# A mixer's second gate product moved to the third block of tokens, and its norm behind the fourth block's gates

## The chip, the cores and the metric

The kernel runs on one core of a Trainium2 chip. The metric is the device time of one execution in microseconds, as a median of several runs; a profile is taken of one further execution. Engines are named as in the profile: PE (TensorE, with PEld for its weight loads), DVE (VectorE), ACT (ScalarE), POOL (GpSimd), SP (SyncE, which only issues DMAs here).

## The reference: what is computed

The kernel is a decoder of six blocks in a row, each followed by a residual sum and a layer norm: a mixer with a state space, a cross attention, a quantized feed-forward part, a causal attention, a recurrent decoder with 128 steps, and a feed-forward part with binary weights. The change touches the first block alone. There the input (16 x 128 tokens of 1024) is projected down to 128, and the same mixer is applied twice in a row, blended with its input, and projected up again. The mixer, cut to what matters:

```
zxbcdt = u @ in_w.T
z, xBC, dt2 = split(zxbcdt)                 # 256, 288, 2 x 4
dt_fw, dt_bw = softplus(dt2 + dt_bias)      # forward and backward in time
xBC = silu(causal_conv(xBC, conv_w, conv_b))            # 7 taps
xs, Bm, Cm = split(xBC)                     # 256, 16, 16
y = shifted scan forward + shifted scan backward        # 16 steps of time
y = y + xs * repeat(xs @ fcD_w.T + D, 64)               # the gate's first product
yz = y * silu(z)                                        # the gate's second product
y = yz * rsqrt(mean(yz ** 2) + 1e-5) * norm_w           # the norm
return y @ out_w.T
```

The scan is over 16 steps, so it is computed as a masked product: for each block of 128 tokens (8 sequences of 16 steps) a 128 x 128 matrix of weights is made for each of 4 heads and multiplied with xs.

## The kernel before, in words

`stage_hydra` cuts the 2048 tokens into 4 quarters of 512 and applies the mixer twice to each: 8 items. They run in 10 rounds of a software pipeline, `for n in range(10)` (line 437). In round n three items are in work: item n is entered (its projections, convolutions and gates: the functions in `first`), item n-1, `inner`, has its four blocks of 128 tokens weighed and summed (`mx.weights(inner, j)`, `mx.summed(inner, j)`), and item n-2, `outer`, is ended (the functions in `last`). The softplus of item n+1 is made by `coming[1]()`. Rounds 2 to 7 hold all three kinds, round 7 without a softplus, round 8 has no item to enter, round 9 only an ending.

The names that matter, with lines of the kernel before:

- `first[0]`, `first[1]`, `first[2]` (`convolved`, lines 249 to 263): a projection by PE (L254), a copy and a scaled copy by ACT (L256, L258), and six steps of the convolution by DVE (L263). They make bc, the first half of xs and the second half of xs.
- `first[3]` (`gates`): the decays by PE (L242), exp by ACT (L244), a sum and a product by POOL (L246, L247), three silus by ACT (L283), two projections by PE with silu by ACT (L287, L288), and the padded copy cpad by POOL (two settings to zero, L291 and L292, and a copy, L293).
- `steps` (`coming[1]`): four small matmuls (L220), the softplus on DVE (L222, L167 to L186, one exp on ACT, L169), and two products by POOL, rf (L234).
- `weights(j)`: two matmuls (L306), masks and their sum by DVE (L308, L310), the weights wt by DVE (L312), two transposes by PE (L316) and a copy xtok by ACT (L318).
- `summed(j)`: four matmuls with wt and xtok (L327) and a copy into y by ACT (L328).
- `last[0]` and `last[1]` are `gated(0)` and `gated(1)`, for the two halves of the 256 channels. `last[2]` is `norm`, `last[3]` projects (L369) and spreads the root over 128 columns (L362, copied by ACT, L364), `last[4]` multiplies the two by DVE (L418, which makes h, the input of the second pass; in the last four endings L426 and a sum by POOL, L427).

```
def gated(c):
    ...
    pf = self.acc()
    for kc in range(2):
        nc.tensor.matmul(pf, w["fc"][...], xs[:, kc, :], start=(kc == 0), stop=(kc == 1))   # L340
    tt = self.t([P, 512], "tt")
    nc.vector.scalar_tensor_tensor(tt, pf, w["D"][:, c:c + 1], xs[:, c, :], ALU.add, ALU.mult)  # L343
    nc.gpsimd.tensor_tensor(tt, tt, y[:, c, :], ALU.add)                                      # L344
    nc.vector.tensor_tensor(y[:, c, :], tt, s["zs"][:, c, :], ALU.mult)                       # L345
    nc.scalar.activation(s["sq"][:, c, :], y[:, c, :], AF.Square)                             # L346
```

`norm` is eight matmuls of a 128 x 128 block of sq with one column of ones (L353; the profile counts 16, as it counts float32 matmuls by passes), one activation by ACT (L355) and one power by POOL (L356). All matmuls here are float32.

What sets the order of the work: `K.ordered` (closed by `order()` at the end of the stage) binds PE and ACT to the order in which the code issues their instructions. DVE and POOL are not bound in this stage; the build orders each of their queues by itself, as it finds operands ready, and that order is then fixed in the program. Each engine runs its queue strictly in order. PSUM has three buffers of 128 x 512 (`acc`) and four of 128 x 256 (`small`), which go round in the order of the code; cpad has two buffers.

Of the kernel before, what the change touches and what calls it, by code (L numbers as in the profile page):

```python
# [69 lines left out]
def column(v):  # L70

    return v.rearrange("(p o) -> p o", o=1)


def spread(v, parts=P):

    return v.rearrange("(o n) -> o n", o=1).to_broadcast([parts, v.shape[0]])
# [301 lines left out]
def stage_hydra(K, xmid, ahead):  # L379

    nc, a = K.nc, K.a
    with ExitStack() as st:
        keep = K.pool(st, "h_keep")
        work = K.pool(st, "h_work")
        ps = K.pool(st, "h_ps", 1, PSUM)
        wdn = K.t(keep, [P, 8, P], "wdn")
        nc.scalar.dma_start(wdn, a["w_downT"].rearrange("(k p) d -> p k d", p=P))
        bdn = K.t(keep, [P, 1], "bdn")
        nc.scalar.dma_start(bdn, column(a["b_down"]))
        xt = []  # L390
        for q in range(4):
            xt.append(K.t(work, [P, 8, 512], "xt", bufs=2))
            for h in range(2):
                nc.sync.dma_start(xt[q][:, 4 * h:4 * h + 4, :],
                                  a["xT"][512 * h:512 * h + 512, q * 512:(q + 1) * 512].rearrange("(k p) n -> p k n", p=P))
            if q == 0:
                w = hydra_weights(K, keep)
        al = K.t(keep, [P, 3], "al")
        nc.scalar.dma_start(al[:, 2:3], spread(a["gate1"]))
        nc.scalar.activation(al[:, 2:3], al[:, 2:3], AF.Sigmoid)  # L400
        nc.vector.tensor_scalar(al[:, 0:1], al[:, 2:3], -1.0, 1.0, ALU.mult, ALU.add)
        nc.vector.tensor_scalar(al[:, 1:2], al[:, 2:3], 1.0, None, ALU.add)
        w["eps"] = K.t(keep, [P, 1], "eps")
        nc.vector.memset(w["eps"], 1e-5)
        mx = Mixer(K, w, work, ps)

        def down(q):
            ph = mx.acc()
            for k in range(8):
                nc.tensor.matmul(ph, wdn[:, k, :], xt[q][:, k, :], start=(k == 0), stop=(k == 7))  # L410
            u = K.t(keep, [P, 512], f"u{q}")
            nc.scalar.activation(u, ph, AF.Gelu, bias=bdn)
            return u

        def between(q):
            def put(po, rr):
                h = h1[q] = K.t(keep, [P, 512], f"h{q}")
                nc.vector.tensor_tensor(h, po, rr, ALU.mult)  # L418
            return put

        def blended(q):
            def put(po, rr):

                t = mx.t([P, 512], "tt")
                nc.scalar.activation(t, u[q], AF.Copy, scale=al[:, 1:2])
                nc.vector.scalar_tensor_tensor(rr, po, al[:, 0:1], rr, ALU.mult, ALU.mult)  # L426
                nc.gpsimd.tensor_tensor(xmid.rearrange("p (l j s) -> p j l s", l=HY_L, s=8)[:, 4 * q:4 * q + 4],  # L427
                                        rr.rearrange("p (j l s) -> p j l s", l=HY_L, s=8),
                                        t.rearrange("p (j l s) -> p j l s", l=HY_L, s=8), ALU.add)
            return put  # L430

        u, h1 = [None] * 4, [None] * 4
        order = K.ordered((mybir.EngineType.Activation, mybir.EngineType.PE))
        inner = outer = None
        for n in range(10):
            s, first = None, []
            ahead(n, mx.acc)
            if n == 0:  # L440
                u[0] = down(0)
                coming = mx.entry(u[0])
                coming[1]()
            if n < 8:
                s, _, first = coming
            if n < 7:
                if n < 3:
                    u[n + 1] = down(n + 1)
                coming = mx.entry(u[n + 1] if n < 3 else h1[n - 3])
            last = []  # L450
            if outer is not None:
                m = n - 2
                last = mx.ending(outer, between(m) if m < 4 else blended(m - 4))
            for j in range(4):
                if last and j < 2:
                    last[j]()
                if inner is not None:
                    mx.weights(inner, j)
                    if j:
                        mx.summed(inner, j - 1)  # L460
                if last and j == 2:
                    last[2]()
                if first:
                    first[j]()
                if n < 7 and j == 1:
                    coming[1]()
                if last and j == 3:
                    last[3]()
            if inner is not None:
                mx.summed(inner, 3)  # L470
            if last:
                last[4]()
            inner, outer = s, inner
        order()
# [1315 lines left out]
def decoder_kernel(tc, a, out):  # L1790
    nc = tc.nc
    K = Ctx(tc, a)
    with ExitStack() as st:
# [11 lines left out]
        with ExitStack() as s1:  # L1805
            xmid = K.t(K.pool(s1, "xmid", side="right"), [P, NT], "xmid")
            rise = Rise(K, K.pool(s1, "c_ahead", side="right"))
            got = []
            steps = {4: lambda bank: rise.load(), 5: lambda bank: got.append(quant_vectors(K, fkeep)), 6: lambda bank: rise.fetch(0),
                     7: lambda bank: rise.fetch(1), 8: rise.fold}  # L1810
            stage_hydra(K, xmid, lambda n, bank: steps[n](bank) if n in steps else None)
            slab = K.pool(st2 := st.enter_context(ExitStack()), "f_w")
            with ExitStack() as s2:
                wf, piece = quant_weights(K, slab, K.pool(s2, "f_raw", 2))
                stage_cross(K, rise, xmid, x1, piece)
# [154 lines left out]
```

## Time and profile before

| what | value |
|---|---|
| median of 3 runs | 3191.89 us (3186.04 to 3192.75) |
| profiled execution, its own time | 3192.77 us |
| its span | 3191.0 us, 70103 instructions, mean clock of TensorE 0.968 |
| round 2 of the mixer stage | 92.47 to 120.40 us of the span |
| round 3 | 120.40 to 149.53 us |
| round 4 | 149.53 to 177.25 us |
| round 5 | 177.25 to 204.96 us |
| round 6 | 204.96 to 232.94 us |
| round 7 | 232.94 to 261.39 us |
| round 8 | 261.39 to 283.63 us |
| first matmul of the next stage | 303.12 us |

A round is counted here from the first matmul of `gated(0)` (L340) to that of the next round. The mixer stage is the first 303 us of the span, a tenth of it; the rest is the five other blocks of the decoder.

How to read it: lines of the profile give the kernel's line number, the engine, the operation, the tiles (output <- inputs), shapes and, in a timeline, the start in microseconds of the span, the duration, and in square brackets how long the engine had been idle before and what released it. "Granted clock" is the share of full speed at which TensorE was clocked. A timeline merges equal instructions that follow each other (x16 is sixteen of them).

### The profile page before, as it was taken

What the parts mean: (1) busy time and instruction counts of PE and PEld (TensorE: products, weight loads), DVE (VectorE), ACT (ScalarE), POOL (GpSimd) and SP (SyncE); (2) the same over time, 40 slices, a digit from 0 to 9 for tenths busy, and PEclk for the clock granted to TensorE, in tenths of its full rate; (3) what the DMA queues carried; (4) which work ended last, traced back from release to release, by engine and by line L of the source; (5) the groups of instructions that cost most, each with busy time, mean ns of one, the idle gap of its engine ahead of it and who ended that gap; (6) DMA issues with size and microseconds to landing.
All of it is one profiled execution on the core that took longest, in us unless ns stands there. A gap on an engine that the chain in (4) does not pass through costs nothing. (4 is left out here: it accounts for less than half of the span.)

```text
span 3191.0 us, 70103 instructions
## 1 busy us (share of the span) xinstructions
PE 2875.3 (90%) x28549; PEld 1615.9 (51%) x28549; DVE 1782.1 (56%) x5099; ACT 1499.6 (47%) x3606; POOL 878.0 (28%) x1096
## 2 busy tenths in 40 slices
PE   6998788799899999999998888888888888888898
PEld 2555455588555555555544444444444444444465
DVE  5785777577244554554434555555555555555555
ACT  3453433455133434442425555555555555565533
POOL 3223755477343333331110111110111111110222
PEclk8887999899999999999999999999999999999999
DMA  5000321221400101024212000101010000000244
GB/s 208 1 1 22 117 71 64 82 70 67 180 27 27 53 26 42 27 66 126 90 38 70 12 22 25 32 25 32 25 32 25 25 19 25 19 19 16 69 112 99
DMA packets 96525, 168.08 MB, mean 53 GB/s; under 512 B 14282, under 2 KB 55115, under 8 KB 96203
## 3 DMA queue, kind: packets, MB, share of 16 engines
q1 hardware_dynamic: 92138, 154.47, 15.2%
q10 hardware_dynamic: 4064, 9.11, 0.7%
q8 instruction: 226, 3.70, 0.5%
q14 instruction: 97, 0.79, 0.1%
HBM read 113.21 MB, written 51.64 MB: 52 GB/s over the span
## 5 line engine op out<-in xcount | busy, mean ns | idle before, releaser
L1177 ACT ACTIVATE th<-pf 128x1024 f32<-128x1024 f32 x381 | 254.2, 740 | 277.2 <-PE pf L1162 277.1
L1305 POOL COPY hist<-gT 128x16 f32<-128x16 f32 x256 | 42.4, 197 | 895.2 <-DVE gT L1304 895.2
L1277 PE MATMUL s<-hb,aD 128*32 128x256 f32 x4096 | 266.9, 387 | 7.9 <-DVE aD L1265 1.0
L854 PE MATMUL p<-xT,ga_Wq 128*128 128x512 f32 x512 | 226.4, 599 | 3.5 <-DMA ga_Wq<-ga_Wq 3.5
L1259 ACT COPY pf<-enc 128x512 f32<-128x512 f32 x381 | 225.5, 592 | 8.0
L928 PE MATMUL p<-ga_Wo,cT 128*128 128x512 f32 x512 | 222.5, 593 | 0.0
L1162 PE MATMUL pf<-R,waf 32*128 32x160 f32 x2032 | 181.4, 426 | 33.7 <-DVE R L1328 33.7
L894 ACT ACTIVATE s<-s,nm 128x128 f32<-128x128 f32 x512 | 197.5, 387 | 27.0 <-DVE nm L891 27.0
L897 POOL TENSOR_TENSOR s<-s,rs 128x512 f32<-128x512 f32 x128 | 133.0, 1039 | 251.7 <-DVE rs L896 246.7
L909 ACT COPY pT<-p 128x512 f32<-128x512 f32 x64 | 37.5, 586 | 269.9 <-PE p L906 269.9
L854 PEld LDWEIGHTS p<-xT,ga_Wq 128*128 128x128 f32 x512 | 96.4, 191 | 132.7 <-issue 119.3
L1195 DVE TENSOR_REDUCE nm<-s 128x1 f32<-128x128 f32 x128 | 37.3, 292 | 219.5 <-PE s L1181 219.5
L928 PEld LDWEIGHTS p<-ga_Wo,cT 128*128 128x128 f32 x512 | 97.1, 190 | 122.3 <-issue 120.5
L1181 PE MATMUL s<-th,vaE 128*32 128x128 f32 x2048 | 82.4, 279 | 78.8 <-ACT th L1177 78.7
L1277 PEld LDWEIGHTS s<-hb,aD 128*32 128x32 f32 x4096 | 95.1, 110 | 109.2 <-DVE aD L1265 86.7
L1297 ACT ACTIVATE fs<-ff,rx 128x384 f32<-128x384 f32 x127 | 73.7, 580 | 147.4 <-DVE rx L1295 147.4
L1162 PEld LDWEIGHTS pf<-R,waf 32*128 32x128 f32 x2032 | 79.3, 182 | 99.3 <-DVE R L1328 74.1
L1181 PE MATMUL ff<-th,vaE 128*32 128x128 f32 x2048 | 108.8, 285 | 8.0
L1109 PE MATMUL p<-ys,qT 128*128 128x512 f32 x256 | 112.3, 595 | 0.1
L1312 PE MATMUL gq<-gs,gT 128*32 128x128 f32 x2032 | 81.8, 279 | 31.8 <-DVE gT L1304 31.8
L95 POOL TENSOR_TENSOR ln_rs<-ln_ve,neghalf 128x1 f32<-128x1 f32 x64 | 37.9, 595 | 261.4 <-DVE ln_ve L89 251.0
L929 DVE TENSOR_TENSOR x<-p,x 128x512 f32<-128x512 f32 x32 | 22.1, 692 | 156.1 <-PE p L928 156.1
(396 smaller groups left out, 6631.3 us busy)
## 6 DMA issues: line engine op xcount, KB each, us to landing
x<-x SPq DMA_DIRECT2D x106, 512.0 KB, 3.6
xt<-xT SPq DMA_DIRECT2D x8, 1024.0 KB, 8.1
x<-x ACTq DMA_DIRECT2D x16, 512.0 KB, 2.6
x<-x SPq DMA_DIRECT2D x128, 64.0 KB, 2.3
xb<-r SPq DMA_DIRECT2D x16, 512.0 KB, 3.0
xb<-xb SPq DMA_DIRECT2D x16, 512.0 KB, 3.9
out<-xb SPq DMA_DIRECT2D x128, 64.0 KB, 2.7
ga_Wo<-ga_Wo SPq DMA_DIRECT2D x2, 2048.0 KB, 12.8
```

Source lines behind the costliest of these rows:

```text
L854: nc.tensor.matmul(pq, lhsT, xT[:, k].rearrange("p i t -> p (i t)"), start=(k == 0), stop=(k == 7))
L894: nc.scalar.activation(s[:, r, :], s[:, r, :], AF.Exp, bias=nm[:, r:r + 1], accum_out=sm[:, r:r + 1])
L897: nc.gpsimd.tensor_tensor(s, s, rs.unsqueeze(2).to_broadcast([P, 4, P]), ALU.mult)
L928: nc.tensor.matmul(po, cT[:, k, :], w["o"][h][:, k, :], start=(k == 0), stop=(k == 7))
L1109: nc.tensor.matmul(py, xT[:, k, b % 4, :], ys[:, k, :], start=(k == 0), stop=(k == 7))
L1162: nc.tensor.matmul(pf[:, k, first:first + n].rearrange("p b t -> p (b t)"), lhs[32 * k:32 * k + 32, :], rhs[32 * k:32 * k + 32, 32 * first ...
L1177: nc.scalar.activation(th.rearrange("p i (k t) -> p i k t", t=32), terms[:, :, first:first + n, :].rearrange("p k i t -> p i k t"), AF.Tanh)
L1181: nc.tensor.matmul(pe[32 * i:32 * i + 32, :], D["va"][:, 31 - b:63 - b], th[:, j, :], start=False, stop=(b % 8 > 3), skip_group_check=True)
L1259: nc.scalar.copy(pf[:, k], D["enc"][:, k])
L1277: nc.tensor.matmul(pg[32 * i:32 * i + 32, :], aD[:, 4 * g + i, :], D["hb"][:, 4 * g + i, :], start=(g == 0), stop=(g == 3), skip_group_che ...
L1297: nc.scalar.activation(fs.rearrange("p c t -> p (c t)"), ff[:, 0:3 * P], AF.Copy, scale=rx)
L1312: nc.tensor.matmul(gq[32 * q:32 * q + 32, :], gT[:, c].rearrange("p e b -> p (e b)"), D["gs"][:, c, q * P:(q + 1) * P], start=False, stop= ...
```

## The change

The diff moves calls in the loop over the four blocks of a round; no instruction is added or taken away.

```
             for j in range(4):
-                if last and j < 2:
-                    last[j]()
+                if last and j in (0, 2):
+                    last[j // 2]()
                 if inner is not None:
                     mx.weights(inner, j)
                     if j:
                         mx.summed(inner, j - 1)
-                if last and j == 2:
-                    last[2]()
                 if first:
                     first[j]()
                 if n < 7 and j == 1:
                     coming[1]()
-                if last and j == 3:
-                    last[3]()
+            if last:
+                last[2]()
             if inner is not None:
                 mx.summed(inner, 3)
             if last:
+                last[3]()
                 last[4]()
```

- The second gate product, `gated(1)`, is issued at the head of block j = 2 and no longer at the head of block j = 1.
- The norm is issued behind the fourth block's `gates`, and no longer between the third block's sum and the third convolution.
- The projection and the spreading of the root come behind the fourth block's sum, and no longer ahead of it.

On PE a round thus runs, before: gate 0, block 0, bc projection, gate 1, block 1, sum 0, xs projection, softplus input, block 2, sum 1, norm, xs projection, block 3, sum 2, decays, two z projections, output projection, root spread, sum 3. And after: gate 0, block 0, bc projection, block 1, sum 0, xs projection, softplus input, gate 1, block 2, sum 1, xs projection, block 3, sum 2, decays, two z projections, norm, sum 3, output projection, root spread. In rounds 8 and 9 the same holds for the parts that they have.

In the built programs DVE and POOL take other orders too. On DVE the steps of the softplus move up among the convolution's steps, L343 and L345 of the second gate stand behind most of the convolutions of bc and of the first half of xs, and L308 of the third and fourth block follow that L345. On POOL the zeroing of the next cpad (L291, L292), which stood behind both gates' L344 and ahead of the power, now stands between the two L344; the products rf (L234) come ahead of the copy into cpad (L293); and the power (L356) is the last of a round. SP's queue keeps its order.

More of the change, by code (lines that the diff above doesn't have):

```diff
@@ L454, in stage_hydra @@
             for j in range(4):
-                if last and j < 2:
-                    last[j]()
+                if last and j in (0, 2):
+                    last[j // 2]()
                 if inner is not None:
@@ L460, in stage_hydra @@
                         mx.summed(inner, j - 1)
-                if last and j == 2:
-                    last[2]()
                 if first:
@@ L466, in stage_hydra @@
                     coming[1]()
-                if last and j == 3:
-                    last[3]()
+            if last:
+                last[2]()
             if inner is not None:
@@ L471, in stage_hydra @@
             if last:
+                last[3]()
                 last[4]()
```

## The prediction

> **What bounds the kernel now.** I read the page's first part, then the mixer stage cut into rounds, then one round as a timeline, then the clock in short windows. The page says that TensorE is the busy engine of the whole kernel:
>
> ```profile
> PE 2875.3 (90%) x28549; PEld 1615.9 (51%) x28549; DVE 1782.1 (56%) x5099; ACT 1499.6 (47%) x3606; POOL 878.0 (28%) x1096
> ```
>
> The change lies in the mixer stage alone, so I cut that into its rounds (a round starts with the first matmul of L340). Columns: time and instructions of PE, PEld, DVE, ACT, POOL, then the granted clock.
>
> ```profile
> 149.53:177.25 27.72, 25.73 (x116) 14.81 (x114) 23.16 (x54) 13.73 (x28) 7.49 (x10) 0.82 0.00 1
> 177.25:204.96 27.71, 26.12 (x116) 15.19 (x115) 23.15 (x54) 13.85 (x28) 7.84 (x11) 0.82 0.00 1
> 261.39:283.63 22.24, 20.35 (x95) 13.28 (x93) 10.14 (x17) 5.07 (x14) 4.80 (x4) 0.69 0.00 0
> ```
>
> A full round takes 27.7 us: PE is busy 26 of it, DVE 23, and the clock is 0.82 on average. The reader should see that two engines are nearly full and that the clock is low. The same round, PE alone, in windows of 3.41 us (busy, then clock):
>
> ```profile
> 156.29:159.70 3.41, 3.41 (x26) 1.00 0.00 0
> 159.70:163.11 3.41, 2.50 (x26) 1.00 0.03 5
> 163.11:166.53 3.42, 3.02 (x8) 0.51 0.00 0
> 166.53:169.94 3.41, 2.73 (x14) 0.50 0.00 0
> 169.94:173.35 3.41, 3.41 (x7) 0.50 0.00 0
> 173.35:176.77 3.42, 3.42 (x16) 0.99 0.00 0
> ```
>
> Cut there, every window is all at full or all at half clock; the falls and rises of the other rounds (about 132.4, 146.1, 190.4, 200.7, 217.7, 228.0) lie on the same grid. [...] The timeline of PE, and what DVE and POOL do meanwhile:
>
> ```profile
> 160.79 0.66 PE L327 MATMUL sm<-wt,xtok 128*64 128x128 f32 x8 [0.91 <-DVE wt L312]
> 161.38 1.95 PE L353 MATMUL sm<-hy_ones,sq 128*128 128x1 f32 x16
> 165.65 1.22 PE L306 MATMUL sm<-cpad,bc 16*128 16x128 f32 x4 [0.41 <-DVE cbm L308]
> 168.16 1.12 PE L327 MATMUL sm<-wt,xtok 128*64 128x128 f32 x8 [0.68 <-DVE wt L312]
> 169.21 2.07 PE L242 MATMUL E<-rf,hy_m 128*128 128x256 f32 x4
> ...
> 156.30 1.27 POOL L344 TENSOR_TENSOR tt<-tt,y 128x512 f32<-128x512 f32 x1 [2.60 <-DVE tt L343]
> 156.47 1.61 DVE L263 SCALAR_TENSOR_TENSOR bc<-raw,hy_cw,bc 64x480 f32<-64x480 f32 x1
> 158.00 0.68 DVE L345 TENSOR_TENSOR y<-tt,zs 128x512 f32<-128x512 f32 x1
> 166.93 0.11 POOL L291 MEMSET cpad<- 16x32 f32 x1 [9.36 <-PE sm L306]
> ```
>
> So a round has a head, 18.6 us, in which PE waits again and again for DVE (it ends when the third block's summing, L327 at 168.16, gets its weights from DVE), and a tail of 9.1 us, to 177.25, in which PE runs alone without a gap. The norm (L353, 16 matmuls of one column, 1.95 us) stands in the head.
>
> **The change, part by part.** Nothing is added or removed: each engine has the same number of instructions, and SP's queue has the same order, so no DMA moves. PE and ACT follow the order of the code; DVE and POOL are ordered by the build, and there the move goes further than the diff. I give times t from the round's first matmul, by rows of round n=4 (row minus 149.53).
>
> *Head, first half.* PE did the second gate product (L340 x4, 1.92 us) while the first block's weights were made. Without it PE is through the second block's L316 at 1.92+0.63+0.37+1.00+0.64+0.37 = 4.9, and must wait for xtok (row 155.03, ends at t=5.85, behind the square of the first gate on ACT): 1.0 us idle. L327 0.58, L254 0.96 and L220 0.88 then end at 8.4.
>
> *Head, second half.* In the built order DVE's reading of the second gate product (L343) stands behind ten convolution steps, and these behind the softplus input, which waits for that L220: 8.5, then 9 steps at 0.57 (the spacing of the interleaved L263 rows) and four small operations, 14.0. L343 takes 0.75, POOL's addition 1.27 (14.8 to 16.1). Row 156.47 shows that a DVE step that starts under it ends 0.5 us after it, 1.61 instead of 0.67; so 16.6. Then come 1.0 us of DVE steps, the gate's last product (L345) at 17.5, and, queued behind it, the masks of the third and the fourth block (L308, 0.41 each, the first ends at 18.6), their sums and the softplus steps between, and the third block's weights, 19.8 to 20.5. PE has done the fourth block's L306 at 13.5 and then waits for the L308 until 18.6: a gap of 5.1 us. The head ends at 20.6 instead of 18.6: +2.0.
>
> POOL zeroes the next cpad (L291) only after that L306, and in the built order this now stands ahead of the second gate's addition. It costs nothing: L306 is through at 13.5, L343 at 14.8. That cover is 1.3 us; what a later L306 costs is a rival below.
>
> *Tail.* At full clock it is L327 0.58, L242 0.94, L287 1.85, L369 1.75, L362 1.06, L327 0.58 = 6.8; before it took 9.1, as 5.2 us ran at half clock (168.16 to 173.35). L353 now stands between L287 and the last L327, where nothing waits for DVE: all 1.95 us count, 8.7. [...] Tail 11.25.
>
> *The root behind it.* The spreading (L362) waits for POOL's power (1.01 us), which now starts later, behind ACT's gates, and behind the rf products and cpad on POOL. ACT reaches the norm's sum (0.28) at 28.3, POOL ends at 29.8; PE gets there at about 30.3. Hidden, by half a microsecond; if that cover goes, up to 1 us a round. In the next round DVE's L418, which makes h, comes later by the last L327 that stood behind L362 (0.58); DVE idles there (2.53 in its row).
>
> *A second fall.* After the rise a window holds L353 whole, with 1.46 us of other matmuls. For such a window the trace has both answers: 285.98 to 289.39 had 1.49 us busy and half clock followed; 408.84 to 412.26 had 1.47 and none did. A low window costs 1.7 us if PE fills it; bounds 0 and 3.4 (two), and I take 0.7, somewhat under one in two.
>
> [...]
>
> *Sum.* A round is 20.6 + 11.25 + 0.7 = 32.55. The five like it (n=2 to 6: 27.93, 29.13, 27.72, 27.71, 27.98) average 28.1: +4.45 each, +22.3. Round n=7 has no softplus, its head ends at 18.4, with tail and one extra matmul (0.33) 30.7 against 28.45: +2.2. Round n=8 (22.24, four windows at half clock) has little DVE work; replayed it is 18.1 at full clock, with gaps of 1.95 and 1.4 us and two or three low windows, some of them in n=9: 0, between -2 and +2. Together +24.5. The next stage starts from the result of the last round, so this passes on. The profiled execution took 3192.77 (span 3191.0 and 1.8 around it), 0.9 above the median of 3191.89; from the median I get 3216.
>
> **The rivals.**
> - *The clock holds (faster).* The gate product fills the sparse stretch between L220 and L353, and PE never leaves full clock: three low windows a round would give back up to 5.1 us. For it: 1.92 us of dense work do move next to the one-column L220. Against: the 5.1 us gap. It decides if the masks come before t = 15.5, leaving a gap under 2 us (1.47 us busy of 3.41 still held). Then a round is 28.1 - 5.1 + 1.95 (the norm in the tail) = 25.0: 5 x -3.1, so 3176.
> - *POOL's zeroing holds up the gate (slower).* If half clock already rules from t = 8, the fourth block's L306 comes at up to 18.5 instead of 13.5, POOL's addition up to 3.7 later, and with it masks and tail: 5 x 8 = +40 and n=7: 3234. For it: the 1.0 us gap and L220 lie together. Against: the window around them still holds L327, L254 and part of a dense L340. It decides from L306 later than 14.7.
> - *Only the move counts.* No second fall and an early rise: 20.6 + 10.4 = 31.0, 5 x 2.9 + 1 - 2 = +13: 3205. This is the lower part of my forecast.
> - *Nothing changes:* head and norm trade places, 3192, within 6 us. It would need a head four microseconds shorter without L353; but DVE ends the head.
>
> **The numbers.** A forecast of slower by rounds of about 32.5 us, with the milder case in it, has 0.78; POOL's zeroing 0.12; nothing 0.04; the clock that holds 0.06. The likeliest gives 3216. The head's replay may be off by 1 us a round (5 in all), the clock by 1.7 a round (9): 3204 to 3232 for it alone, and with the zeroing rival's end the range is 3203 to 3234. The runs before spread over 6.7 us, 0.2%, which is what can be told from no change: faster 0.06, same 0.04, slower 0.90.
>
> **What would show it.** In the new trace: rounds of 31 to 34 us; PE idle for 4 to 6 us before the third or fourth block's L316, released by DVE; POOL's L291 done before the second L344 is ready; L353 without a wait behind L287 and L362 with hardly one; DVE idle for some 6 us at the end of a round; and half clock in every tail. Rounds under 28 us, or a clock of 1.00 through the tail, would make the prediction wrong; so would DVE reading the second gate product well before t = 14.

## The result, and the profile after

The changed kernel takes 3203.01 us (median of 4 runs, 3202.04 to 3205.57) against 3189.35 us for the kernel before in runs on the same chip (3186.04 to 3192.75): a ratio of 1.0044, with a 95% interval of 1.0027 to 1.0061. It is slower by 13.7 us. The profiled execution took 3202.16 us, 9.4 more than the one before.

The page's first part, to be held against the one line shown before: PE is busy for 17 us less, although the kernel takes longer, and the other engines hardly moved. So PE waits more.

```profile
PE 2858.0 (89%) x28549; PEld 1604.2 (50%) x28549; DVE 1777.5 (56%) x5099; ACT 1500.1 (47%) x3606; POOL 881.3 (28%) x1096
```

The mixer stage cut into its rounds, the same columns as before (time and instructions of PE, PEld, DVE, ACT, POOL, then the granted clock); rounds n=4, n=5 and n=8:

```profile
151.43:182.09 30.66, 24.39 (x116) 14.33 (x115) 22.46 (x54) 13.84 (x27) 8.56 (x10) 0.83 0.00 1
182.09:212.78 30.69, 24.42 (x116) 14.35 (x115) 22.47 (x54) 13.84 (x27) 8.56 (x10) 0.83 0.00 1
...
272.39:296.88 24.49, 21.15 (x92) 13.04 (x93) 9.34 (x17) 4.71 (x13) 4.81 (x4) 0.72 0.00 0
```

| round | n=2 | 3 | 4 | 5 | 6 | 7 | 8 | sum |
|---|---|---|---|---|---|---|---|---|
| before | 27.93 | 29.13 | 27.72 | 27.71 | 27.98 | 28.45 | 22.24 | 191.16 |
| after | 30.44 | 30.61 | 30.66 | 30.69 | 30.71 | 28.90 | 24.49 | 206.50 |

The rounds hold +15.3 us, so the whole loss is where the change is. Round 2 starts 2.1 us earlier in the new profile, the next stage starts 13.5 us later (its first matmul at 316.59 instead of 303.12), and all that follows took 4.1 us less in this execution, which is why the two profiled executions differ by 9.4 only.

One round (n=4) as a timeline, start, duration, engine, line; in brackets the idle time before and what ended it:

```profile
157.29 0.66 PE L327 MATMUL sm<-wt,xtok 128*64 128x128 f32 x8 [0.97 <-ACT xtok L318]
...
164.19 0.71 PE L306 MATMUL sm<-cpad,bc 16*128 16x128 f32 x4
164.96 0.12 POOL L291 MEMSET cpad<- 16x32 f32 x1 [9.46 <-PE sm L306]
165.18 0.74 DVE L343 SCALAR_TENSOR_TENSOR tt<-acc,hy_D,xs 128x512 f32<-128x512 f32 x1
165.99 1.54 POOL L344 TENSOR_TENSOR tt<-tt,y 128x512 f32<-128x512 f32 x1 [0.86 <-DVE tt L343]
167.90 0.68 DVE L345 TENSOR_TENSOR y<-tt,zs 128x512 f32<-128x512 f32 x1
168.61 0.41 DVE L308 TENSOR_TENSOR cbm<-sm,hy_m 128x256 f32<-128x256 f32 x1
169.07 0.69 PE L316 MATMUL sm<-ident,xs 128*128 128x128 f32 x2 [4.17 <-DVE cbm L308]
170.07 0.68 DVE L312 TENSOR_TENSOR wt<-e,cb 128x512 f32<-128x512 f32 x1
170.89 1.12 PE L327 MATMUL sm<-wt,xtok 128*64 128x128 f32 x8 [1.13 <-ACT xs L258]
...
177.02 1.84 PE L353 MATMUL sm<-hy_ones,sq 128*128 128x1 f32 x16
...
179.51 1.02 POOL L356 TENSOR_TENSOR ve<-ve,neghalf 128x4 f32<-128x4 f32 x1
181.20 1.05 PE L362 MATMUL acc<-ident,ve 128*128 128x128 f32 x8
182.91 0.69 DVE L418 TENSOR_TENSOR h<-acc,rr 128x512 f32<-128x512 f32 x1 [6.76 <-ACT rr L364]
```

The reader sees the new wait: DVE reaches the second gate product (L343) 13.75 us into the round, the gate's last product (L345) at 16.5, and only then the masks (L308) for which PE has waited 4.17 us. The third block's sum (L327 at 170.89, t = 19.46) ends the head; before it was at t = 18.63. The profile puts the 1.13 us ahead of it down to ACT's L258, but the sum reads nothing that L258 makes: its weights are DVE's L312, which ended at 170.75, 0.14 us before it (0.15 in the kernel before). So DVE ends the head here too. Behind it the norm (L353) now counts in full: the tail is 11.2 us, before it was 9.1. PE's clock in windows of 3.41 us (PE busy, clock):

```profile
163.11:166.53 3.42, 1.79 (x8) 1.00 0.00 0
166.53:169.94 3.41, 0.69 (x2) 0.51 0.00 0
169.94:173.35 3.41, 2.46 (x11) 0.50 0.02 5
173.35:176.77 3.42, 3.42 (x6) 0.50 0.00 0
176.77:180.18 3.41, 3.41 (x27) 0.99 0.00 0
```

Three windows are at half clock (166.57 to 176.81), as before (163.19 to 173.43), but 1.5 us later in the round (from t = 15.1 instead of 13.7); after the rise the clock is 1.00 to the end of the round (176.81 to 182.09).

### The profile page after: what moved, and what is told of

Read it like the earlier page. It is cut to its first block, busy times and chain, and to the rows that moved or that the text cites. A ratio compares the mean times of both kernels' runs of the same rounds, so it can differ in the third digit from the quotient of the medians.

```text
span 3200.4 us, 70097 instructions
## 1 busy us (share of the span) xinstructions
PE 2858.0 (89%) x28549; PEld 1604.2 (50%) x28549; DVE 1777.5 (56%) x5099; ACT 1500.1 (47%) x3606; POOL 881.3 (28%) x1096
## 4 chain that ended last, share of the span: by engine, by line
PE 66%; DVE 13%; ACT 9%; POOL 4%; DMA 3%; issue 3%; SPq 1%; POOLq 0%; DVEq 0%; ACTq 0%
PE p L853 8%; PE s L1276 8%; PE pf L1161 7%; ACT th L1176 7%; PE p L927 6%; PE p L1108 4%; PE acc L701 3%; PE m L1724 3%; PE gq L1311 3%; PE ff L1291 3%; PE p L905 2%; DMA x<-x 2%; PE s L1220 2%; PE p L866 2%; PE o L708 1%
## 5 line engine op out<-in xcount | busy, mean ns | idle before, releaser
L893 ACT ACTIVATE s<-s,nm 128x128 f32<-128x128 f32 x512 | 197.5, 388 | 27.3 <-DVE nm L890 27.3
```

The source lines that it names most:

```text
L893: nc.scalar.activation(s[:, r, :], s[:, r, :], AF.Exp, bias=nm[:, r:r + 1], accum_out=sm[:, r:r + 1])
```

## The experiments

"Before" and "changed" are the two kernels. Rounds are n=2 to 6 of the profiled execution; "rounds 2 to 8" is the sum of seven rounds less the 191.16 us of the kernel before; "median" is the run's median less that of the kernel before on the same chip.

| run | rounds n=2 to 6, us | rounds 2 to 8 | median | ratio, 95% interval |
|---|---|---|---|---|
| changed | 30.44, 30.61, 30.66, 30.69, 30.71 | +15.3 | +13.7 | 1.0044 (1.0027 to 1.0061) |
| e1_extra_norm | 32.97, 30.24, 30.48, 33.83, 33.99 | +28.8 | +28.4 | 1.0091 (1.0074 to 1.0108) |
| e2_half_norm | 30.09, 30.14, 30.14, 30.14, 30.14 | +12.3 | +6.4 | 1.0029 (1.0017 to 1.0041) |
| e3_cpad3 | 30.52, 30.66, 30.68, 30.71, 30.70 | +15.5 | +16.0 | 1.0052 (1.0036 to 1.0069) |
| e4_norm_only | 29.15, 29.51, 29.14, 29.14, 29.14 | +5.0 | +3.0 | 1.0009 (1.0000 to 1.0018) |
| e5_gate_only | 33.64, 33.78, 33.78, 33.78, 33.92 | +31.1 | +26.9 | 1.0084 (1.0065 to 1.0104) |
| e6_project_back | 30.79, 30.88, 30.86, 30.87, 30.88 | +13.1 | +10.0 | 1.0036 (1.0017 to 1.0054) |
| e7_after_warm | 29.83, 30.77, 30.75, 30.76, 30.76 | +11.4 | +9.1 | 1.0026 (1.0014 to 1.0038) |
| e8_before_warm | 27.69, 27.80, 30.68, 30.98, 30.75 | +6.8 | +7.1 | 1.0016 (1.0007 to 1.0026) |
| e9_after_warm_rf_dve | 29.23, 29.27, 29.22, 29.26, 29.27 | +6.2 | +5.8 | 1.0019 (1.0010 to 1.0029) |
| e10_after_rf_dve | 29.48, 29.96, 30.33, 30.53, 30.62 | +13.1 | +14.3 | 1.0042 (1.0027 to 1.0057) |
| e11_before_z_first | 28.95, 27.46, 27.45, 27.55, 27.77 | -3.3 | -2.8 | 0.9990 (0.9981 to 1.0000) |
| e12_before_z_first_warm | 25.79, 27.53, 27.42, 27.38, 27.33 | -6.4 | -6.2 | 0.9983 (0.9974 to 0.9993) |

In the mixer stage every stretch at half clock, from 85 us of the span on and in every trace, lasts 3.41 us (279.21 to 282.62 in the changed kernel) or a multiple of it (6.83, 10.24, 13.65, up to 20.48 in e1). In rounds n=2 to 6 of the changed kernel half clock begins every 30.72 us (at 105.13, 135.85, 166.57, 197.29 and 228.01), a ninth of which is 3.413, and the rounds come ever closer to that length. A first theory followed, the author's guess that the grid of these stretches locks the round; e1 and e2 were made for it.

**The two halves of the change, e4 and e5.** e4 keeps both gate products where they were and moves the norm and the projection alone; e5 moves the gate alone.

```
e4 (from the changed kernel)                e5 (from the kernel before)
-  if last and j in (0, 2):                 -  if last and j < 2:
-      last[j // 2]()                       -      last[j]()
+  if last and j < 2:                       +  if last and j in (0, 2):
+      last[j]()                            +      last[j // 2]()
```

> Both gate products stand where they were before; norm and projection come as late as in the changed kernel. Theory: DVE ends the head as before, at about 18.6 us, and only the tail grows by the norm (1.95) and keeps its low windows: rounds of 29 to 30, total 6 to 13 us above the kernel before, so the norm alone has about half of the loss or more. If the grid decides, single rounds of 27.3 or 30.7. Rival (the second gate product's place is what costs): rounds of 28, total within 3 us of the kernel before.

> Only the second gate product is moved to the third block; the norm stands behind the third block's sum as before, so it must now wait on PE for the squares of the second gate, which come at about t = 17, and the third convolution's projection, the fourth block and its sum stand behind it. Theory: head of 21 to 24 us, tail of 7 to 9, rounds of 30 to 32, total 13 to 22 us above the kernel before: slower than the norm moved alone. Rival (the gate's move is free, the norm in the tail is the loss): rounds of 28 to 28.5, total within 3 us of the kernel before.

e4: 29.14, inside the range for the rounds, but the total is 3.0 above, less than the 6 to 13 expected. The norm alone costs 1.4 us a round (29.14 against 27.7); the gate's move adds the other 1.6. Without the norm among its work the head even ends earlier, at t = 17.8 (L327 at 195.84 in a round that starts at 178.05), and the end of the round is then set by POOL, not by PE's instructions:

```profile
203.10 2.06 POOL L234 TENSOR_TENSOR rf<-ld,hy_mc 128x512 f32<-128x512 f32 x2 [0.96 <-DVE ld L229]
205.13 1.02 POOL L356 TENSOR_TENSOR ve<-ve,neghalf 128x4 f32<-128x4 f32 x1
...
206.20 1.16 PE L362 MATMUL acc<-ident,ve 128*128 128x128 f32 x8 [0.41 <-POOL ve L356]
```

That is why its rounds are 29.14 with one, two or three windows at half clock. e5: the direction was right and the forecast too small (30 to 32 a round, 13 to 22 in total; it was 33.8 and 26.9). In the timeline of its round n=4 (start 158.97) the norm, at its old place, stops PE's queue for 5.8 us until the second gate's squares are made, the third block's sum comes at t = 24.7, and four windows are at half clock:

```profile
170.75 0.38 PE L353 MATMUL sm<-hy_ones,sq 128*128 128x1 f32 x2
176.91 3.15 PE L353 MATMUL sm<-hy_ones,sq 128*128 128x1 f32 x14 [5.78 <-ACT sq L346]
...
183.67 1.12 PE L327 MATMUL sm<-wt,xtok 128*64 128x128 f32 x8
```

So the effects don't add (1.4 and 6.1 alone, 2.9 together): a later gate is only bearable with the norm behind it.

**POOL's zeroing, e3.** A third buffer: `self.t([16, 4, P + 16], "cpad", bufs=3)`.

> A third buffer for the padded copy frees POOL's zeroing from the fourth block's small matmuls. Theory (zeroing costs nothing, DVE reaches the second gate product later than it): rounds of 30.7 as in the changed kernel, total within 2 us of it. Rival (POOL's zeroing holds up the gate): POOL's second addition starts earlier, the head shortens by up to a microsecond and the total falls by 3 to 6 us.

Rounds as in the changed kernel, the median 2.4 us further from the kernel before, within the spread of its four runs. But the edit did not do what it was made for: in this trace, too, the zeroing waits for the fourth block's L306 (L291 at 165.94 in a round that starts at 152.40, t = 13.54; in the changed kernel 13.53). So the run tests nothing. The changed kernel's own trace settles the question: POOL ends its zeroing at 165.14 and then idles 0.86 us until DVE's L343 releases the addition (L344 at 165.99). The zeroing holds nothing up.

**The projection, e6.** `last[3]()` stands ahead of `mx.summed(inner, 3)` again.

> As the changed kernel, with the projection and the spreading of the root ahead of the fourth block's sum again. Theory: the same work in the tail; the spreading now waits some tenths of a microsecond for POOL's power, the grid takes that up: rounds of 30.6 to 30.8, total within 2 us of the changed kernel. Rival (the wait for the power counts): rounds of 31.3, total 3 to 4 us above the changed kernel.

Rounds of 30.87, a tenth above the forecast: the spreading waits 0.18 to 0.34 us for the power in rounds n=4 to 6. The total is 3.7 below that of the changed kernel, outside the 2 us expected, which the rounds 2 to 7 don't explain; 2.9 of it is round 8 (21.58 instead of 24.49). What sets round 8 stays open: it was 20.4 to 25.8 us long over the runs, with one to six windows at half clock.

**A longer and a shorter norm, e1 and e2.** e1 adds four one-column matmuls of sq to the norm in rounds 2 to 7, into the unused half of its PSUM tile; e2 makes `for c in range(2)` of the norm a `range(1)` there, so that the squares of the other 128 channels are left out of the norm.

> Theory of the lock: the tail's loss of half clock ends on a grid of 3.413 us, so that a delay inside the round is halved in each round and the rounds settle at nine windows, 30.72 us. Four one-column matmuls more per round (eight passes, 0.92 us) in rounds 2 to 7 then vanish: rounds of 30.6 to 30.8 as in the changed kernel, total within 2 us of it. Rival, the plain sum by which the tail is as long as its instructions: rounds of 31.6, total 5.5 us above the changed kernel.

> In rounds 2 to 7 the norm sums the squares of the first 128 channels only (the other half is left out), which takes 0.92 us of PE out of the tail. Plain sum: rounds of 29.8, total 5.5 us below the changed kernel. Theory of the lock: at full clock the round is then 26.9 us, just below the span of about 27.3 to 29.0 that nine windows hold, so rounds still near 30.7 or, where the grid lets them go, unequal ones between 28 and 30.7; total 0 to 9 us below the changed kernel. Equal rounds of 29.8 would speak against the lock.

e1 fits neither: two rounds of 30.2 to 30.5 and three of 33 to 34. In the long ones the clock falls a second time. PE in round n=5, by windows, and the norm of rounds n=4 and n=5 as a timeline:

```profile
206.95:210.37 3.42, 3.42 (x25) 1.00 0.00 0
210.37:213.79 3.42, 3.42 (x15) 0.50 0.01 2
213.79:217.20 3.41, 3.41 (x10) 0.50 0.00 0
```
```profile
177.55 0.95 PE L354 MATMUL sm<-hy_ones,sq 128*128 128x1 f32 x8
178.36 1.93 PE L357 MATMUL sm<-hy_ones,sq 128*128 128x1 f32 x16
...
208.15 0.95 PE L354 MATMUL sm<-hy_ones,sq 128*128 128x1 f32 x8
208.96 2.26 PE L357 MATMUL sm<-hy_ones,sq 128*128 128x1 f32 x16
211.15 1.12 PE L327 MATMUL sm<-wt,xtok 128*64 128x128 f32 x8
```

The window ahead of the fall has no gap at all, but 2.2 us of it (208.15 to 210.37) were one-column matmuls, and 1.2 us others. In the changed kernel's window 176.77:180.18 they were 1.84 and 1.57, and the clock held. Within e1 itself it goes in order: in round n=4 the window that ends at 179.66 had no gap either, with 2.1 us of one-column matmuls (from 177.55 on) and 1.3 of others, and the clock held, as it did with 1.9 in n=3; with 2.2, 2.4 and 2.7 (n=5, 6 and 2) it fell. Two windows at half clock cost 33.83 - 30.48 = 3.35 us, twice the 1.7 that the prediction had put on one. So 0.92 us more of the norm cost up to 3.4 a round.

e2 excludes the plain sum (29.8). Its equal rounds look like a lock, but at 30.14, not at 30.72, and the timeline of round n=5 names another cause:

```profile
205.55 2.31 POOL L234 TENSOR_TENSOR rf<-ld,hy_mc 128x512 f32<-128x512 f32 x2 [0.22 <-DVE ld L229]
...
209.28 1.02 POOL L356 TENSOR_TENSOR ve<-ve,neghalf 128x4 f32<-128x4 f32 x1
210.35 1.16 PE L362 MATMUL acc<-ident,ve 128*128 128x128 f32 x8 [1.05 <-POOL ve L356]
```

PE, now with time to spare, waits 1.05 us for POOL's power, which stands behind the products rf, the copy into cpad and the sum `both`. The power ends at t = 29.10, exactly as in the changed kernel, however soon PE is ready. With DVE's and POOL's orders as in the changed kernel, this chain alone makes a round of 30.14. The theory of the lock fell; a new one took its place: *two limits tie*. PE at half clock needs 30.7, and ACT's gates with POOL's queue up to the power need 30.14.

**Holding the clock, e7 and e8.** Dummy matmuls of 256 columns, whose results nobody reads, go into the second half of a `small` tile, which is made twice as wide for them:

```
-        return self.K.t(self.ps, [P, 2, P], "sm", bufs=4)
+        return self.K.t(self.ps, [P, 4, P], "sm", bufs=4)
...
+        for _ in range(fill):
+            nc.tensor.matmul(pc[:, 2:4, :]..., w["in"][:, 0:P], w["m"]..., start=True, stop=True)
         cbm = self.t([P, 2, P], "cbm")
...
-                    mx.weights(inner, j)
+                    mx.weights(inner, j, 7 if last and n < 8 and j == 3 else 0)      # e7
```

> The changed kernel with seven dummy matmuls (256 columns, 3.3 us of PE at full clock, results unread) in rounds 2 to 7 between the fourth block's two kinds of matmuls, in the gap of 4.2 us that DVE sets. Theory: the clock stays at 1.00 through the tail, each round loses the 3 us of half clock: rounds of 27.7, total 16 to 18 us below the changed kernel, about 3185. Rival (the tail is long for another reason, such as waits for DVE or POOL that half clock hides): rounds above 29.5.

> The kernel before with dummy matmuls (256 columns, 0.47 us each at full clock, results unread) in rounds 2 to 7: two ahead of the third block's transposes, three behind the norm, three ahead of the fourth block's transposes. Theory: the head stays as DVE sets it, 18.6 us, the clock holds and the tail takes 6.8 instead of 9.1: rounds of 25.4, total 13 to 16 us below the kernel before, under both kernels. Rival (the dummies push the head back by themselves, or too few to hold the clock): rounds of 27.3 or more.

Both missed, and both by the rival's side. e7's first round ran at full clock throughout and the others at 0.94:

```profile
90.84:120.67 29.83, 24.77 (x129) 15.20 (x128) 22.17 (x53) 13.84 (x27) 8.79 (x10) 1.00 0.00 1
120.67:151.44 30.77, 26.23 (x131) 16.24 (x130) 22.48 (x54) 13.61 (x27) 8.34 (x10) 0.94 0.00 1
```

and still, but for the first, they are no shorter than in the changed kernel, as PE waits 1.26 us for the power ahead of its spreading. (In this build POOL copies cpad ahead of the rf products, which puts the power 0.6 us later than in the changed kernel; e2 is the cleaner run for the size. The total is 4.5 below that of the changed kernel, mostly by round 8, 21.57 instead of 24.49 as in e6.) e8 shows the same of the kernel before. Its first two rounds run at full clock and take 27.69 and 27.80, no less than at 0.82:

```profile
91.32:119.01 27.69, 25.09 (x131) 15.64 (x130) 22.55 (x53) 14.16 (x27) 7.97 (x9) 1.00 0.00 1
119.01:146.81 27.80, 25.21 (x133) 15.75 (x131) 23.25 (x54) 13.96 (x28) 8.69 (x10) 1.00 0.00 1
```
```profile
145.16 1.13 PE L367 MATMUL acc<-ident,ve 128*128 128x128 f32 x8 [2.53 <-ACT zs L288]
```

Here the spreading waits 2.53 us for ACT's silu of the first z projection, which frees its PSUM buffer and which stands on ACT behind the silu of the third convolution's result. Some of this wait is made by the dummies, as DVE's masks had to wait for them too: 0.42 us in these two rounds, 2.0 in rounds n=4 to 6, which have two windows at half clock. So e8 does not show by itself how long a round of the kernel before would be at full clock.

**Both limits off, e9 to e12.** e9 and e10 move the products rf to DVE, which idles at the end of a round (`nc.vector.tensor_tensor(r, ...)` for `nc.gpsimd.tensor_tensor(r, ...)`, L234); e9 has e7's dummies besides and two more ahead of the third block's sum. e11 and e12 start from the kernel before and put the silus of the z projections ahead of the silu of the second half of xs; e12 has dummies besides, in tiles for which no other engine waits.

```
e11
-            for c in (2, 0, 1):
-                ... silu of bc, xs 0, xs 1
+            silu(2)
+            silu(0)
             s["zs"] = self.t([P, 2, 512], "zs", bufs=3)
             for c in range(2):
                 ... projection and silu of z
+            silu(1)
```

> The changed kernel with both suspected limits of its tail taken off: seven dummy matmuls in the gap ahead of the fourth block's transposes and two more ahead of the third block's sum (they hold TensorE's clock), and the two products rf on DVE, which idles at the end of a round, so that POOL's queue reaches the power 2 us earlier. Theory of two limits that tie (half clock on PE, and ACT's gates with POOL's queue up to the power): only with both gone the round shrinks, to 28.5 to 29.5, where ACT's gates and the power alone hold the spreading of the root; total 8 to 13 us below the changed kernel. Rival (one limit only, the clock or POOL's queue): the kernel with the dummies alone kept 30.76, so if the clock is not a limit at all, this is as fast as the next run without dummies.

> The changed kernel with the two products rf on DVE and no dummies. Theory of two limits that tie: POOL's power comes 2 us earlier, but PE at half clock reaches the spreading no earlier: rounds of 30.4 to 30.8, total within 2 us of the changed kernel. Rival (POOL's queue is the limit): rounds of 29 to 30, total 5 to 9 us below the changed kernel.

> The kernel before with one swap in the gates on ACT: the silus of the two z projections come ahead of that of the second half of xs, which waits for the third convolution; so the PSUM buffer that the spreading of the root takes over is free about 1.5 us earlier. DVE's and POOL's orders in the rounds stay. Theory of two limits that tie in the kernel before too: PE at half clock ends the round as before, rounds of 27.4 to 27.8, total within 3 us of the kernel before. Rival (ACT's gates are the limit): rounds of 26.5 or less.

> The same swap, and dummy matmuls in rounds 2 to 7 where PE waits for DVE, so placed that no other engine waits for them: two ahead of the second block's sum, three ahead of the norm, three ahead of the third block's sum. Theory: both limits are gone, the clock holds, the head stays 18.6 and the tail takes 6.8 to 7.8: rounds of 25.4 to 26.5, total 8 to 15 us below the kernel before and below every other kernel here. Rival (the clock falls all the same, or DVE, busy for 23.2 us of a round, holds it): rounds of 27.3 or more, total within 3 us of the kernel before.

e9: the rounds n=2 to 7 at full clock, the first five 29.25 long, as expected; the total is 7.8 below that of the changed kernel, just short of the 8 to 13:

```profile
121.28:150.55 29.27, 25.89 (x134) 15.85 (x133) 24.11 (x56) 13.74 (x27) 6.29 (x8) 1.00 0.00 1
150.55:179.77 29.22, 25.90 (x134) 15.86 (x133) 24.06 (x56) 13.74 (x27) 6.36 (x8) 1.00 0.00 1
```
```profile
178.78 1.16 PE L367 MATMUL acc<-ident,ve 128*128 128x128 f32 x8 [1.23 <-POOL ve L361]
```

e10, with POOL's queue relieved and the clock left alone, comes back to 30.62 after shorter first rounds, and its median is that of the changed kernel. One limit off gives 0 to 0.6 us a round (e10, e7, e2), both off 1.45; even then the spreading waits 1.23 us for the chain through ACT's gates and the power.

e11: but for the first, rounds of 27.45 to 27.77, a fifth of a microsecond under those before; -2.8 us, with an interval that ends at no change. That is within what was expected, and the rival is excluded. e12 holds the clock in its first round only, and that round takes 25.79, as the theory has it:

```profile
93.46:119.25 25.79, 25.25 (x132) 15.44 (x130) 22.58 (x53) 13.98 (x27) 5.77 (x8) 1.00 0.00 1
119.25:146.78 27.53, 26.99 (x133) 16.61 (x131) 23.32 (x54) 13.78 (x28) 9.62 (x12) 0.94 0.00 1
146.78:174.20 27.42, 26.88 (x132) 16.51 (x130) 23.32 (x54) 13.77 (x28) 8.00 (x11) 0.94 0.00 1
```

In the others one window falls to half clock just where three dummies stand, these then take 2.9 us instead of 1.6 and push the third block's sum from t = 18.7 to 20.2. By the rounds the forecast (25.4 to 26.5) was met once in five, and the other four lie on the rival's side (27.3 or more). The total of 3182.01 us, short of the forecast too, is nevertheless the lowest of all, 6.2 below the kernel before, an interval wholly under 1: this version beats both kernels. That 25.8 can be held for all rounds was not shown.

## Why the prediction was right, and where it was not

*The direction and the mechanism* were right: slower, by DVE reading the second gate late. L343 at t = 13.75 (forecast 14.0), gaps on PE of 0.97 and 4.17 us (1.0 and 5.1), and a third of 1.13 that was not forecast, the zeroing free, no wait ahead of L353 or L362, DVE idle for 6.76 us at the end, half clock in every tail. The time, 3203.01, lies at the very low end of the range (3203 to 3234), and the likeliest value, 3216, was far off: a loss of 24.5 forecast, 13.7 measured, 15.3 in the rounds. What came is nearest to the milder case that the forecast held within it (no second fall: rounds of 31.0, 3205); the rounds of 30.4 to 30.7 lie just under the 31 to 34 that were to show it. Term by term:

- *Head, second half* (+2.0): measured +0.83. The step that failed is "Then come 1.0 us of DVE steps": DVE ran its step ahead of the one that stretched under POOL's addition (L263 at 166.59, 1.28 us, where the one before it took 0.57; the addition ended at 167.53), not behind it, so L345 came at 16.5 instead of 17.5 and everything after it a microsecond sooner. This is 5 x 1.15 = 5.8 of the 9 us.
- *A second fall* (0.7): measured 0 in all five rounds, 3.5 of the 9 us. The hazard itself was real: e1 shows it, at 3.35 a round, with 0.92 us more of one-column matmuls.
- *Tail* 11.25: measured 11.2 (170.89 to 182.09 in round n=4). The 2.55 us in it beyond the 8.7 of its instructions at full clock are a term that no run shows; measured was half clock in the first 5.92 us of that tail and full clock in the other 5.28, a mean of 0.74. Right in size, but the reading behind it was incomplete, see below.
- *Round n=7* +2.2, measured +0.45; *round n=8* 0, measured +2.25. They cancel; the second is not explained.
- *POOL's zeroing* as a rival: excluded by the trace, in which POOL idles 0.86 us between the zeroing and the addition (a cover of 1.3 was forecast); e3 could not test it.
- *The root behind it*, "Hidden, by half a microsecond; if that cover goes, up to 1 us a round": the power ended at t = 29.10 and the spreading began at 29.77, a cover of 0.67. When PE was made faster the cover went at once, and PE waited 1.05 (e2), 1.26 (e7) and 1.23 us (e9).

That last term carries the lesson that I had missed. The prediction read the tail as one "in which PE runs alone without a gap" and put up to 5.1 us a round on the lost clock, so the rival in which the clock holds got 25.0 a round and 3176. e9 has the clock at 1.00 in the rounds n=2 to 7, and its rounds are 29.25, not 25.0: the head stays at 19.4 us, as DVE's masks come as late as in the changed kernel (the rival asked for masks before t = 15.5; here they start at 17.2), and 1.23 us are the wait for the power. In the kernel before, e8's two rounds at full clock took 27.7, with 0.42 us of delay by their own dummies. Less work on PE won the changed kernel some 0.6 us a round (30.71 to e2's 30.14); what the clock alone would win, with POOL's order unchanged, no run shows. In the kernel before, the first z silu ended 0.3 us ahead of the spreading (L362 at 175.68), which was to be read in ACT's timeline (two silus, 0.53 each, start of the first 174.87), and in rounds n=2 and n=6 the spreading already waited for it:

```profile
118.75 1.13 PE L362 MATMUL acc<-ident,ve 128*128 128x128 f32 x8 [0.34 <-ACT zs L288]
...
174.87 1.06 ACT L288 ACTIVATE zs<-acc 128x512 f32<-128x512 f32 x2
...
231.30 1.13 PE L362 MATMUL acc<-ident,ve 128*128 128x128 f32 x8 [0.29 <-ACT zs L288]
```

The prediction set the gap ahead of the masks (5.1 us forecast, 4.17 measured) against a clock that holds. In the changed kernel the clock did fall 1.7 us into that gap (at 166.57; PE idles from 164.90 on), after a window with 1.79 us busy; but in e1 it fell after a window in which PE was busy for 3.42 of 3.42 us. The second fall, put at 0.7, came in none of the five rounds of the changed kernel; its window behind the rise (176.77:180.18) had no gap, but e1's had none either.

## What to carry to other kernels

An engine that is busy without a gap is not thereby the limit: ask when the other operands of its last steps were ready, and by how little; here a tail at half clock hid chains through ACT and POOL that ended 0.3 and 0.7 us earlier, so making TensorE faster alone gave little (0 to 0.6 us a round in the changed kernel), and only both together paid. Before moving an instruction on one engine, replay the queues of those that read its result: the loss here was DVE's masks, queued behind a gate product that came late, and a norm that used to fill waits and now stands where nothing waits. Look out for long runs of one-column matmuls: in e1 the windows of 3.41 us that held 2.2, 2.4 and 2.7 us of them were followed by half clock, those with 1.9 and 2.1 were not. That mixing them with dense ones helps was not tried.

## What the runs showed of the hardware

- The clock of TensorE fell after a window with no idle time: 2.2 us of one-column matmuls and 1.2 us of others (e1, round n=5, 206.95:210.37), while it held after 2.1 and 1.3 (e1, round n=4) and after 1.84 and 1.57 (the changed kernel, 176.77:180.18). In e8, windows without a gap that held 1.95 us of one-column matmuls were followed by full clock twice (those that start at 102.91 and 130.22) and by half clock three times (157.52, 188.24, 218.96); the three ahead of half clock also held two transposes (0.38 us). No run varied one of these alone.
- The rounds of the changed kernel (30.44, 30.61, 30.66, 30.69, 30.71) and of e10 (29.48 to 30.62) creep up towards 30.72 us, with about half of the distance left after each round; 30.72 us is also the distance from one beginning of half clock to the next in these rounds of the changed kernel. That the one makes the other was not shown: the run made to test it, e1, answered with second falls instead, and other rounds settled elsewhere (30.14 in e2, 30.87 in e6) where a wait for POOL ended them.
